# A selective scan whose carried state enters through its input: constant starts, a ring of four input slots, the state copied by another engine

## The chip, the cores and the metric

The kernel runs on one core of a Trainium2 chip. A core has engines that run side by side and wait for each other by semaphores: TensorE (PE, matrix products), VectorE (DVE), ScalarE (ACT), GpSimd (POOL) and SyncE (SP), whose queue issues most of the transfers (DMAs). The metric is the device time of one execution in microseconds (us); lower is better.

## The reference

Two layers over an image of 4 x 512 channels x 64 x 64, so 4 sequences of 4096 positions. The first layer normalizes, cuts the 512 channels into four chunks of 128 and runs one Mamba block over each of the 16 sequences; the second is linear attention. What matters here is the scan of the Mamba block:

```python
A = -jnp.exp(A_log)
def step(h, inp):
    dt_t, B_t, C_t, x_t = inp
    dA = jnp.exp(dt_t[:, :, None] * A)
    h = dA * h + (dt_t * x_t)[:, :, None] * B_t[:, None, :]
    y = jnp.einsum('bds,bs->bd', h, C_t)
    return (h, y)
h0 = jnp.zeros((Beff, D_INNER, D_STATE), x.dtype)
```

D_INNER is 256 and D_STATE is 16, so each position has 4096 states, and the recurrence runs over 4096 positions.

## The kernel before

**Steps.** The work is cut into tiles of T = 512 positions: 4 images x 8 tiles x 4 chunks = 128 steps (b, t, c), in that order. A step has two halves (e = 0, 1; 128 inner channels each), and a half has 8 slots: SLOTS = 16 slots a step, 2048 in all. A slot does two scans of 128 rows x 512 positions; two slots, jj = 0 and 1, make a pair, which is one group q of four states for all 128 channels of the half. The global slot number is g.

**What a slot needs.** Both halves' dt and dt*x go to DRAM (`d_rows`, line 629) and come back spread over the partitions as `d_all` (`spread`, line 633: eight transfers of 256 KB each time, called in slot 1 for half 1 and in slot 9 for half 0 of the next step). `b_all` is one group's rows of B, broadcast over partitions by four transfers of 64 KB (`b_row`, line 692); `c_sb` is the tail of the rows of C (`c_tail`, line 697, four of 16 KB). ACT forms dA = exp(dt * A) into one of three PSUM banks (`decay`, line 708, three scans ahead). POOL forms bx = (dt*x) * B for two scans at once (`drive`, line 717), two slots ahead, into one of three tiles.

**What a slot does** (`slot`, line 725). DVE runs two scans (line 739), h = dA * h + bx along the 512 positions. The scan's starting value is 0.0 in the first tile of an image and a column of `st` later, the state left by the tile before. At the end of a pair POOL copies the last column of h into `st` (line 750) and multiplies the last 128 positions of h by C, in place (line 751); DVE multiplies the first 384 (`product`, line 759), one scan into the next pair; PE sums the states of a channel (`fold_states`, line 761).

**Order.** Inside `manual_schedule` every engine and SP's queue work through their instructions in the order in which the code issues them. A queue whose first instruction must wait holds back all behind it. `after()` (line 1108) places the other work of a step in its slots: the next step's products, `spread`, `gate` (POOL, line 780, slots 1 and 9), `to_rows` (POOL, line 624, slot 4, the product dt*x), the norms and the attention, which are generators that advance a piece at a time as PE's budget allows. In the transfers this gives, per pair: `b_row` for a pair three ahead in the even slot, `c_tail` in the odd one, and `spread` after the `c_tail` of slots 1 and 9. Tiles that share a tag and a number of buffers reuse each other's memory; a new use waits for the old one's last reader.

**Norms.** `layer_norm` (line 419) and `layer_scale` (line 450) work on one tile of positions. Means and variances come from sums over partitions on PE; the temporary tiles all have the tag `sq`, four buffers.

Of the kernel before, what the change touches and what calls it, by code (L numbers as in the profile page):

```python
# [8 lines left out]
F32 = mybir.dt.float32  # L9
# [15 lines left out]
def kernel(  # L25
# [136 lines left out]
    ident = wk.tile([P, P], F32, tag="sq", name="ident", bufs=4)  # L162
# [62 lines left out]
    w_x = wk.tile([P, DI], F32, tag="bx", name="w_x", bufs=3)  # L225
# [37 lines left out]
    a_sb = rows(a_log, wk.tile([P, NH, NST], F32, tag="sq", name="a_sb", bufs=4))  # L263
# [9 lines left out]
    b_qk = wk.tile([P, C], F32, tag="bx", name="b_qk", bufs=3)  # L273
# [15 lines left out]
    a_k = wk.tile([P, NH, KS, NQ], F32, tag="sq", name="a_k", bufs=4)  # L289
# [96 lines left out]
    def mean_of(sums, what, when, stop=True):  # L386

        got = wk.tile([P, T], F32, tag="sq", name=f"got_{what}", bufs=4)
# [14 lines left out]
    def over_deviation(v, var, name):  # L403
        rs = wk.tile([P, T], F32, tag="sq", name=f"rs_{name}", bufs=4)
# [14 lines left out]
    def layer_norm(v, name):  # L419
# [6 lines left out]
        mu = yield from mean_of(sums, f"mu_{name}", "one ahead")  # L426
# [4 lines left out]
        sqs = []  # L431
        for c in range(NC):
            sqs.append(wk.tile([P, T], F32, tag="sq", name=f"sq_{name}_{c}", bufs=4))
            nc.scalar.activation(sqs[c], v[:, c, :], AF.Square)
            if c == 1:
                yield "free"
        yield from room()
        sums = work_bank(f"var_sums_{name}")
        sums_into(sums, sqs, range(NC))
        var = yield from mean_of(sums, f"var_{name}", "two ahead")  # L440
# [9 lines left out]
    def layer_scale(v, name):  # L450
# [8 lines left out]
        mu = yield from mean_of(sums, f"mu_{name}", None)  # L459
        mu2 = wk.tile([P, T], F32, tag="sq", name=f"mu2_{name}", bufs=4)  # L460
# [8 lines left out]
        sqs = [None] * NC  # L469

        def part(c):
            sqs[c] = wk.tile([P, T], F32, tag="sq", name=f"sq_{name}_{c}", bufs=4)
            nc.scalar.activation(sqs[c], v[:, c, :], AF.Square, bias=about)
# [12 lines left out]
        var = yield from mean_of(sums, f"var_{name}", "two ahead", False)  # L486
# [80 lines left out]
    def shifted_end(f, name):  # L567
# [4 lines left out]
        d2 = small.tile([P, NC], F32, tag="d2", name=f"d2_{name}")  # L572
# [110 lines left out]
    b_all, c_all, c_sb, dAs, bxs, hs, ys = {}, {}, {}, {}, {}, {}, {}  # L683
# [8 lines left out]
    def b_row(g):  # L692
        n, e, q, _ = place(g)
        b_all[g // JJ] = wk.tile([P, T], F32, tag="b_all", name=f"b_all_{g}", bufs=3)
# [22 lines left out]
    def drive(g):  # L717

        n, e, q, jj = place(g)
        bxs[g] = wk.tile([P, 2, T], F32, tag="bx", name=f"bx_{g}", bufs=3)  # L720
        nc.gpsimd.tensor_tensor(  # L721
            bxs[g], fs[n]["d_all", e][:, 1, jj * 2 : jj * 2 + 2, :], bc(b_all[g // JJ], 2), ALU.mult
        )

# [515 lines left out]
```

## Time and profile before

| | |
|---|---|
| median of 3 runs | 7956.4 us (7953.15 to 7964.96) |
| profiled execution | 7963.09 us, span 7961.4 us |
| first scan / last scan begins | 122.4 us / 7492.2 us |
| DVE busy | 6977.7 us (88%) |
| POOL busy | 6880.5 us (86%) |
| PE busy | 6453.6 us (81%) |
| ACT busy | 5507.6 us (69%) |
| the hardware DMA queue q1 | 1222.32 MB, 61.1% of the 16 engines' span |
| chain that ended last, by engine | DVE 33%, PE 21%, ACT 15%, DMA 12%, issue 8%, SPq 6%, POOL 6% |

In a group's row of the profile stand the line of the code, the engine, the operation, the tiles written and read, the shapes and the count; then the busy time of the group in us, the mean duration of one in ns, and the time its engine sat idle just before such instructions, with what ended most of that. A row of a timeline is: start in us, time covered in us, engine, line, operation, tiles, shape, and how many instructions were merged into the row; the bracket is idle time and what ended it. Instructions that follow each other on one engine overlap by some 0.05 to 0.1 us, so what one more costs is read from start to start. SPq rows are SP issuing transfers; a row of four issues that waits inside shows as a longer row. A row of waits is: who waited, for what, us in total, times, the longest in us.

### The profile page before, as it was taken

The page shows a single profiled execution, that of the slowest core. Times are in us where ns is not written, and L with a number is a line of the kernel's source. Part 1 is how long each engine was busy: PE and PEld are TensorE (multiplying, and loading weights), DVE is VectorE, ACT ScalarE, POOL GpSimd, SP SyncE. Part 2 cuts the span into 40 slices and gives each one's busy share as a digit, 9 for nine tenths or more (in the row PEclk, how much of TensorE's full clock was granted, in tenths as well). Part 3 has the DMA queues.
Part 4 walks back from the last instruction along what each step waited for, and adds up shares of the span by engine and source line. Part 5 has one row for each costly group of instructions (what it writes and reads, how often), then busy time and mean ns, then how long its engine had stood idle before and what let it go on. Part 6 is the DMA issues. An engine that isn't in the chain of part 4 may idle for free.

```text
span 7961.4 us, 90563 instructions
## 1 busy us (share of the span) xinstructions
PE 6453.6 (81%) x24835; PEld 2120.0 (27%) x24880; DVE 6977.7 (88%) x5766; ACT 5507.6 (69%) x8321; POOL 6880.5 (86%) x4597
## 2 busy tenths in 40 slices
PE   5676777677789888888788888898688888888599
PEld 1121212112223222322222223332122332322144
DVE  5999999999999999989999999998999999988600
ACT  4667777777777777767777777677777777777421
POOL 4999999999999899989999899898999999889600
PEclk7888888888899999998899999899899999999799
DMA  5666666666666666777766666677666666676402
GB/s 154 167 168 166 151 155 159 160 155 167 169 179 162 151 163 159 174 189 175 174 155 171 171 157 161 155 185 189 156 167 163 161 161 159 145 194 180 112 32 90
DMA packets 829184, 1265.87 MB, mean 159 GB/s; under 512 B 183912, under 2 KB 317560, under 8 KB 816384
## 3 DMA queue, kind: packets, MB, share of 16 engines
q1 hardware_dynamic: 804736, 1222.32, 61.1%
q0 software_dynamic: 16896, 33.56, 2.4%
q10 hardware_dynamic: 7040, 4.20, 0.2%
q8 instruction: 195, 3.19, 0.2%
q14 instruction: 317, 2.60, 0.1%
HBM read 1052.78 MB, written 206.57 MB: 158 GB/s over the span
## 4 chain that ended last, share of the span: by engine, by line
DVE 33%; PE 21%; ACT 15%; DMA 12%; issue 8%; SPq 6%; POOL 6%; POOLq 0%; ACTq 0%; DVEq 0%
DVE h L739 22%; DVE h L759 9%; DMA d_all<-d_rows 7%; ACT dA L713 5%; PE pq L124 5%; POOL bx L721 4%; PE pc L124 4%; SPq L688 3%; PE y L124 3%; PE pr L124 3%; SPq L639 2%; DMA c_sb<-c_rows 2%; ACT xz L1048 2%; PE po L124 2%; ACT L1048 1%
## 5 line engine op out<-in xcount | busy, mean ns | idle before, releaser
L721 POOL TENSOR_TENSOR bx<-d_all,b_all 128x1024 f32<-128x1024 f32 x2048 | 4824.7, 2367 | 213.3 <-DVE h L739 195.1
L739 DVE TENSOR_TENSOR_SCAN h<-dA,st,bx 128x512 f32<-128x512 f32 x3584 | 4358.9, 1264 | 358.7 <-ACT dA L713 159.0
L713 ACT ACTIVATE dA<-d_all,a_t 128x512 f32<-128x512 f32 x4096 | 2752.9, 687 | 1568.5 <-DVE h L739 1521.8
L759 DVE TENSOR_TENSOR h<-h,c_all 128x1536 f32<-128x1536 f32 x1024 | 1767.5, 1726 | 0.1
L751 POOL TENSOR_TENSOR h<-h,c_sb 128x512 f32<-128x512 f32 x1024 | 1300.2, 1270 | 190.2 <-DMA c_sb<-c_rows 95.2
L124 PE MATMUL y<-h,fold 128*32 128x512 f32 x8192 | 1271.2, 696 | 71.6 <-POOL h L751 67.4
L124 PE MATMUL c_all<-parts,sel 128*128 128x384 bf16 x1024 | 369.9, 361 | 1123.3 <-DVE h L759 1121.7
L124 PE MATMUL pc<-xn,w_cv 128*128 128x512 f32 x2048 | 1045.7, 645 | 122.8 <-DVE xn L414 62.1
L124 PE MATMUL pq<-w_qk,xa 128*128 128x512 f32 x2048 | 965.5, 604 | 7.9 <-issue 5.3
L739 DVE TENSOR_TENSOR_SCAN h<-dA,bx 128x512 f32<-128x512 f32 x512 | 591.2, 1203 | 90.0 <-ACT dA L713 65.1
L124 PEld LDWEIGHTS <-sel 128*128 128x128 bf16 x1280 | 127.1, 99 | 1762.2 <-DVE h L759 1562.5
L124 PEld LDWEIGHTS pc<-xn,w_cv 128*128 128x128 f32 x2048 | 389.5, 201 | 747.1 <-issue 424.7
L124 PEld LDWEIGHTS pq<-w_qk,xa 128*128 128x128 f32 x2048 | 398.6, 196 | 439.6 <-issue 422.4
L124 PE MATMUL pr<-xb,m 128*128 128x512 f32 x1024 | 485.3, 612 | 7.5 <-DMA xb<-x 3.6
L124 PE MATMUL pp<-xn,w_pr 128*128 128x512 f32 x1024 | 477.7, 597 | 4.8 <-DVE xn L414 4.8
L124 PEld LDWEIGHTS y<-h,fold 128*32 128x32 f32 x8192 | 170.6, 114 | 644.0 <-issue 344.9
L124 PE MATMUL y<-xz,dg 32*32 32x512 f32 x2048 | 337.3, 734 | 0.0
L781 POOL TENSOR_TENSOR xz<-xz 128x512 f32<-128x512 f32 x256 | 325.7, 1272 | 9.2 <-ACT xz L778 9.2
L832 ACT ACTIVATE kq<-pq 128x512 f32<-128x512 f32 x256 | 150.5, 588 | 259.9 <-PE pq L124 259.2
L124 PE MATMUL pd<-xz,w_xp 128*128 128x512 f32 x512 | 323.4, 764 | 7.8 <-ACT xz L1048 7.8
L628 POOL TENSOR_TENSOR dt<-dt,xz 128x1024 f32<-128x1024 f32 x128 | 302.3, 2361 | 24.7 <-ACT dt L620 24.6
L124 PE MATMUL pz<-xn,w_z 128*128 128x512 f32 x512 | 275.4, 631 | 11.7 <-ACT xz L608 8.2
(179 smaller groups left out, 6034.1 us busy)
## 6 DMA issues: line engine op xcount, KB each, us to landing
d_all<-d_rows SPq DMA_DIRECT2D x2048, 256.0 KB, 6.7
b_all<-b_rows SPq DMA_DIRECT2D x4096, 64.0 KB, 2.2
d_rows<-dt SPq DMA_DIRECT2D x256, 512.0 KB, 3.6
c_sb<-c_rows SPq DMA_DIRECT2D x4096, 16.0 KB, 1.8
xs<-in_x_dram SPq DMA_DIRECT2D x32, 1024.0 KB, 6.3
xn<-in_x_dram SPq DMA_DIRECT2D x32, 1024.0 KB, 6.2
xr<-in_x_dram POOLq DMA_DIRECT2D x32, 1024.0 KB, 10.7
x<-xr SPq DMA_DIRECT2D x32, 1024.0 KB, 4.2
```

The costliest lines, as they stand in the source:

```text
L124: nc.tensor.matmul(out_, lhsT, rhs, **how)
L628: nc.gpsimd.tensor_tensor(f["both"][:, 1], f["both"][:, 0], f["xz"][:, 0], ALU.mult)
L639: nc.sync.dma_start(d[k * BLK : (k + 1) * BLK, v], src)
L688: nc.sync.dma_start(dst[k * BLK : (k + 1) * BLK, :], rows_[q * KS + k, :].partition_broadcast(BLK))
L713: nc.scalar.activation(dAs[k], fs[n]["d_all", e][:, 0, j, :], AF.Exp, scale=a_t[:, e, j, q : q + 1])
L721: nc.gpsimd.tensor_tensor(bxs[g], fs[n]["d_all", e][:, 1, jj * 2 : jj * 2 + 2, :], bc(b_all[g // JJ], 2), ALU.mult)
L739: nc.vector.tensor_tensor_scan(h[:, j, :], dAs.pop(2 * g + i), bxs[g][:, i, :], 0.0 if t == 0 else st[:, c, e, q, j : j + 1], ALU.mult, AL ...
L751: nc.gpsimd.tensor_tensor(h[:, :, CUT:], h[:, :, CUT:], bc(c_sb.pop(g // JJ), NJ), ALU.mult)
L759: nc.vector.tensor_tensor(own, own, bc(c_all.pop(g // JJ), NJ), ALU.mult)
L781: nc.gpsimd.tensor_tensor(f["xz"][:, 1, e, :], f["xz"][:, 1, e, :], f["xz"][:, 0, e, :], ALU.mult)
L832: nc.scalar.activation(qk[i], pq, AF.Relu)
L1048: nc.scalar.activation(fs[n]["xz"], fs[n]["xz"], AF.Silu)
```

## The change

Every scan starts at the constant 0.0. The state of the tile before enters instead through bx: the first column of a pair's bx gets `exp(A * dt_first) * st` added, which is what the scan would have made of its starting value. For this a small tile `carry` (128 x 32) is formed per half, in steps with t > 0: `carry_over` (POOL, A times the first column of dt), `carry_decay` (ACT, Exp) and `carry_on` (POOL, times `st`); then one POOL add of 128 x 4 elements follows the second drive of every pair. bx becomes one tile of four slots, `drive` runs three slots ahead (DRIVE = 3), `st` is copied by ACT. Memory for the fourth slot comes from `b_all` (two buffers in place of three, loaded in the odd slot behind `c_tail`, for the pair two ahead), from `sq` (three fixed tiles `sqb` in place of four rotating ones, so that one norm's variance sums are split in two) and from two small tiles. `spread` moves from slot 1 to slot 0 and from slot 9 to slot 7.

```diff
-    b_all, c_all, c_sb, dAs, bxs, hs, ys = {}, {}, {}, {}, {}, {}, {}
+    b_all, c_all, c_sb, dAs, hs, ys = {}, {}, {}, {}, {}, {}
+    RING, DRIVE = 4, 3
+    bx = const.tile([P, RING, 2, T], F32, tag="bx", name="bx")
+    carry = const.tile([P, NH, NJ, NQ], F32, tag="carry", name="carry")
...
     def b_row(g):
         n, e, q, _ = place(g)
-        b_all[g // JJ] = wk.tile([P, T], F32, tag="b_all", name=f"b_all_{g}", bufs=3)
+        b_all[g // JJ] = wk.tile([P, T], F32, tag="b_all", name=f"b_all_{g}", bufs=2)
         for_states(b_all[g // JJ], fs[n]["b_rows"], q)
...
     def drive(g):
 
         n, e, q, jj = place(g)
-        bxs[g] = wk.tile([P, 2, T], F32, tag="bx", name=f"bx_{g}", bufs=3)
         nc.gpsimd.tensor_tensor(
-            bxs[g], fs[n]["d_all", e][:, 1, jj * 2 : jj * 2 + 2, :], bc(b_all[g // JJ], 2), ALU.mult
+            bx[:, g % RING], fs[n]["d_all", e][:, 1, jj * 2 : jj * 2 + 2, :],
+            bc(b_all[g // JJ], 2), ALU.mult,
         )
+        if jj == JJ - 1 and steps[n][1]:
+            if q == 0:
+                carry_on(g)
+            r = (g - jj) % RING
+            first = bx[:, r : r + JJ, :, 0].rearrange("p r i -> p (r i)")
+            nc.gpsimd.tensor_tensor(first, first, carry[:, e, :, q], ALU.add)
+
+    def carry_over(g):
+
+        n, e, _, _ = place(g)
+        nc.gpsimd.tensor_tensor(
+            carry[:, e], a_t[:, e],
+            fs[n]["d_all", e][:, 0, :, 0].unsqueeze(2).to_broadcast([P, NJ, NQ]), ALU.mult,
+        )
+
+    def carry_decay(g):
+        _, e, _, _ = place(g)
+        nc.scalar.activation(carry[:, e], carry[:, e], AF.Exp)
+
+    def carry_on(g):
+        n, e, _, _ = place(g)
+        nc.gpsimd.tensor_tensor(
+            carry[:, e], carry[:, e], st[:, steps[n][2], e].rearrange("p q j -> p j q"), ALU.mult
+        )
+
+    def starts_half(g, last):
+
+        return g < last and g % (SLOTS // NH) == 0 and steps[g // SLOTS][1] > 0
 
     def slot(g, last, after):
         n, e, q, jj = place(g)
         b, t, c = steps[n]
-        if g + 2 < last:
-            drive(g + 2)
+        if starts_half(g + DRIVE + 1, last):
+            carry_over(g + DRIVE + 1)
+        if g + DRIVE < last:
+            drive(g + DRIVE)
         if jj == 0:
-            if g + 3 * JJ < last:
-                b_row(g + 3 * JJ)
             hs[g // JJ] = wk.tile([P, NJ, T], F32, tag="h", name=f"h_{g}", bufs=2)
-        elif g + 1 < last:
-            c_tail(g + 1)
+        else:
+            if g + 1 < last:
+                c_tail(g + 1)
+            if g + 1 + 2 * JJ < last:
+                b_row(g + 1 + 2 * JJ)
         h = hs[g // JJ]
         for i in range(2):
             j = jj * 2 + i
             nc.vector.tensor_tensor_scan(
-                h[:, j, :], dAs.pop(2 * g + i), bxs[g][:, i, :],
-                0.0 if t == 0 else st[:, c, e, q, j : j + 1], ALU.mult, ALU.add,
+                h[:, j, :], dAs.pop(2 * g + i), bx[:, g % RING, i, :], 0.0, ALU.mult, ALU.add,
             )
+            if i == 1 and jj == JJ - 1:
+                nc.scalar.copy(st[:, c, e, q, :], h[:, :, T - 1])
...
-        del bxs[g]
+        if starts_half(g + DRIVE, last):
+            carry_decay(g + DRIVE)
         if jj == JJ - 1:
-            nc.gpsimd.tensor_copy(st[:, c, e, q, :], h[:, :, T - 1])
             nc.gpsimd.tensor_tensor(
                 h[:, :, CUT:], h[:, :, CUT:], bc(c_sb.pop(g // JJ), NJ), ALU.mult
             )
...
-    for g in range(JJ, 3 * JJ, JJ):
-        b_row(g)
+    b_row(JJ)
     c_row(0)
-    for g in range(2):
+    for g in range(DRIVE):
         drive(g)
+    b_row(2 * JJ)
...
-                    if s == 1:
+                    if s == 0:
                         spread(f, 1, nm)
-                        if before is not None:
-                            gate(before, 1)
+                    if s == 1 and before is not None:
+                        gate(before, 1)
...
+                    if s == 7 and nxt is not None:
+                        spread(nxt, 0, names[n + 1])
                     if s == 9:
                         gate(f, 0)
-                        if nxt is not None:
-                            spread(nxt, 0, names[n + 1])
```

In the norms (left out here but for the core):

```diff
-    ident = wk.tile([P, P], F32, tag="sq", name="ident", bufs=4)
+    sqb = const.tile([P, 3, T], F32, tag="sqb", name="sqb")
+    ident = sqb[:, 0, 0:P]
...
-        sqs = []
-        for c in range(NC):
-            sqs.append(wk.tile([P, T], F32, tag="sq", name=f"sq_{name}_{c}", bufs=4))
+        sqs = [sqb[:, i, :] for i in (1, 2, 0, 1)]
+        for c in range(2):
             nc.scalar.activation(sqs[c], v[:, c, :], AF.Square)
-            if c == 1:
-                yield "free"
+        yield "free"
         yield from room()
         sums = work_bank(f"var_sums_{name}")
-        sums_into(sums, sqs, range(NC))
-        var = yield from mean_of(sums, f"var_{name}", "two ahead")
+        sums_into(sums, sqs, (0, 1))
+        for c in range(2, NC):
+            nc.scalar.activation(sqs[c], v[:, c, :], AF.Square)
+        yield "free"
+        sums_into(sums, sqs, (2, 3))
+        var = yield from mean_of(sums, f"var_{name}", "two ahead", 0)
```

More of the change, by code (lines that the diff above doesn't have):

```diff
@@ L224 @@
     w_cv = const.tile([P, NTAP, DI], F32, tag="w_cv", name="w_cv")
-    w_x = wk.tile([P, DI], F32, tag="bx", name="w_x", bufs=3)
+    w_x = wk.tile([P, DI], F32, tag="res", name="w_x", bufs=2)
     nc.scalar.dma_start(w_x, in_w[:, 0:DI])
@@ L262 @@
     skd = const.tile([P, BLK], F32, tag="skd", name="skd")
-    a_sb = rows(a_log, wk.tile([P, NH, NST], F32, tag="sq", name="a_sb", bufs=4))
+    a_sb = rows(a_log, sqb[:, 1, 0 : NH * NST].rearrange("p (e s) -> p e s", e=NH))
     w_op = const_rows(op_w, "w_op")
@@ L272 @@
     bqk = const.tile([P, C], BF16, tag="bqk", name="bqk")
-    b_qk = wk.tile([P, C], F32, tag="bx", name="b_qk", bufs=3)
+    b_qk = wk.tile([P, C], F32, tag="res", name="b_qk", bufs=2)
     nc.vector.memset(b_qk, 0.0)
@@ L286 @@
         nc.vector.tensor_copy(bqk[r, :], b_qk[r, :])
-    a_k = wk.tile([P, NH, KS, NQ], F32, tag="sq", name="a_k", bufs=4)
+    a_k = sqb[:, 2, 0 : NH * NST].rearrange("p (e k q) -> p e k q", e=NH, k=KS)
     nc.scalar.activation(a_k, a_sb.rearrange("p e (q k) -> p e k q", k=KS), AF.Exp)
@@ L384, in sums_into, with mean_of @@
             )
-    def mean_of(sums, what, when, stop=True):
-        got = wk.tile([P, T], F32, tag="sq", name=f"got_{what}", bufs=4)
+    def mean_of(sums, what, when, at, stop=True):
+        got = sqb[:, at, :]
         def take():
@@ L403, in over_deviation @@
     def over_deviation(v, var, name):
-        rs = wk.tile([P, T], F32, tag="sq", name=f"rs_{name}", bufs=4)
+        rs = sqb[:, 2, :]
         def root():
@@ L425, in layer_norm @@
         sums_into(sums, [v[:, c, :] for c in range(NC)], range(NC))
-        mu = yield from mean_of(sums, f"mu_{name}", "one ahead")
+        mu = yield from mean_of(sums, f"mu_{name}", "one ahead", 0)
         yield "wide"
@@ L458, in layer_scale @@
         sums_into(sums, [v[:, c, :] for c in range(NC)], range(NC))
-        mu = yield from mean_of(sums, f"mu_{name}", None)
-        mu2 = wk.tile([P, T], F32, tag="sq", name=f"mu2_{name}", bufs=4)
+        mu = yield from mean_of(sums, f"mu_{name}", None, 0)
+        mu2 = sqb[:, 0, :]
         def square():
@@ L468, in layer_scale @@
         yield from until(squared)
-        sqs = [None] * NC
+        sqs = [sqb[:, i, :] for i in (1, 2, 1, 2)]
         def part(c):
-            sqs[c] = wk.tile([P, T], F32, tag="sq", name=f"sq_{name}_{c}", bufs=4)
             nc.scalar.activation(sqs[c], v[:, c, :], AF.Square, bias=about)
@@ L485, in layer_scale @@
         sums_into(sums, sqs, (2, 3))
-        var = yield from mean_of(sums, f"var_{name}", "two ahead", False)
+        var = yield from mean_of(sums, f"var_{name}", "two ahead", 1, False)
         mm(var, minus_first.to_broadcast([P, P]), mu2, start=False, stop=True)
@@ L571, in shifted_end @@
         nc.vector.tensor_scalar(mv, mv, 1.0 / L, None, ALU.mult)
-        d2 = small.tile([P, NC], F32, tag="d2", name=f"d2_{name}")
+        d2 = small.tile([P, NC], F32, tag="d2", name=f"d2_{name}", bufs=1)
         nc.vector.tensor_tensor(d2, mv[:, :, 0], mv[:, :, 0], ALU.mult)
@@ L896, in attention @@
         nc.gpsimd.memset(kqn, 0.0)
-        nrm = small.tile([P, NC], F32, tag="nrm", name=f"nrm_{b}")
+        nrm = small.tile([P, NC], F32, tag="nrm", name=f"nrm_{b}", bufs=1)
         nc.vector.tensor_reduce(nrm, kq, AX.X, ALU.add)
```

## The prediction

> **What bounds the kernel now.** I read the groups by cost first, then the waits, then the timelines of DVE, POOL and SP's queue over one stretch.
>
> ```profile
> span 7961.4 us, 90563 instructions
> L721 POOL TENSOR_TENSOR bx<-d_all,b_all 128x1024 f32<-128x1024 f32 x2048 | 4824.7, 2367 | 213.3 <-DVE h L739 195.1
> L739 DVE TENSOR_TENSOR_SCAN h<-dA,st,bx 128x512 f32<-128x512 f32 x3584 | 4358.9, 1264 | 358.7 <-ACT dA L713 159.0
> L739 DVE TENSOR_TENSOR_SCAN h<-dA,bx 128x512 f32<-128x512 f32 x512 | 591.2, 1203 | 90.0 <-ACT dA L713 65.1
> ```
>
> The loop of 2048 slots runs from 122 to 7494 us, 7371 us, 57.6 per step of 16 slots; about 590 us lie outside it. Inside, DVE is busy 6914 us and POOL 6867: two engines at 93%, each idle for some 460 to 510 us. A change must help both, or it moves the bound to the other.
>
> ```profile
> 4024.81 1.73 DVE L759 TENSOR_TENSOR h<-h,c_all 128x1536 f32<-128x1536 f32 x1
> 4026.45 4.80 DVE L739 TENSOR_TENSOR_SCAN h<-dA,st,bx 128x512 f32<-128x512 f32 x4
> 4031.17 1.73 DVE L759 TENSOR_TENSOR h<-h,c_all 128x1536 f32<-128x1536 f32 x1
> ```
> ```profile
> 4021.44 2.35 POOL L721 TENSOR_TENSOR bx<-d_all,b_all 128x1024 f32<-128x1024 f32 x1 [0.16 <-DVE h L739]
> 4023.78 0.19 POOL L750 COPY st<-h 128x4 f32<-128x4 f32 x1
> 4024.05 1.27 POOL L751 TENSOR_TENSOR h<-h,c_sb 128x512 f32<-128x512 f32 x1
> 4025.28 2.36 POOL L721 TENSOR_TENSOR bx<-d_all,b_all 128x1024 f32<-128x1024 f32 x1
> 4027.81 2.37 POOL L721 TENSOR_TENSOR bx<-d_all,b_all 128x1024 f32<-128x1024 f32 x1 [0.17 <-DVE h L739]
> ```
>
> A pair of slots (one b_all tile, four scans) takes DVE 6.36 us (4024.81 to 4031.17) without a gap. POOL needs start to start 2.34 + 0.27 + 1.23 + 2.36 = 6.2 us, and waits 0.17 for the scan that frees a bx buffer. They are level.
>
> SP's queue is the third clock. After every spread (eight d_all transfers of 256 KB, twice per step) the transfers behind it are issued slowly:
>
> ```profile
> 4024.05 1.76 SPq L688 DMA_DIRECT2D b_all<-b_rows  x4
> 4025.90 1.76 SPq L688 DMA_DIRECT2D c_sb<-c_rows  x4
> 4027.76 3.70 SPq L639 DMA_DIRECT2D d_all<-d_rows  x8
> 4031.56 3.79 SPq L688 DMA_DIRECT2D b_all<-b_rows  x4
> 4036.26 4.07 SPq L688 DMA_DIRECT2D c_sb<-c_rows  x4
> 4040.43 1.91 SPq L688 DMA_DIRECT2D b_all<-b_rows  x4
> ```
> ```profile
> SPq L688 <- DMA d_all<-d_rows: 1555.2, 1736, 3.9
> ```
>
> Four issues cost 1.76 us when nothing holds them, 3.8 and 4.07 behind a spread; 1736 waits over 256 spreads are about seven of the next eight. So the first four behind a spread are out 7.6 us after it began (4035.35), the next four 12.6 us after (4040.33). This costs almost nothing today, since b_all is loaded long ahead.
>
> **The change, part by part.**
>
> *Scans.* 3584 scans lose the st operand. Start to start: 4.72 us for four with st (4026.45 to 4031.17) is 1.18 each; in the first tile, where the start is already constant, four take 143.72 to 148.20, 4.48, or 1.12. 60 ns x 3584 = 215 us off DVE's busy time, which the means (1264 less 1203, 61 ns) repeat. That is the whole possible gain; it is time only where DVE ends last.
>
> *st copy.* POOL loses 1024 copies of 0.27 us start to start (4023.78 to 4024.05): 276 us. ACT gains them and 224 carry_decay; ACT has no 128x4 copy, so between the 0.19 of its accumulator read and the 0.47 of a 32x384 cast; I take 0.22: 275 us. ACT idles 1522 us before L713, waiting for the scans, which hides it; without that cover each copy would hold back a decay, 275 us. The tail product L751 overwrites h, so it now waits for ACT's copy. POOL's copy waited for the scan only 79 times in 1024, 79 us, so the scan is normally long over; I price this at 0 to 150 us and take 20. The Trainium skill (ScalarE: Activation LUTs, "What ACT_TABLE_LOAD costs") has 186 ns + 0.833 ns per element, an estimate of 0.19 us for this copy; no run here shows it, and by it the sum would stay.
>
> *Small adds on POOL.* 896 adds, 224 carry_over, 224 carry_on. No small POOL multiply or add is shown; the rows at 512 elements (1270 ns) and 1024 (2367) extrapolate to 0.17 at none, and the copy has 0.20. Below is 0.15 (a pad copy's pitch, 4010.13 to 4010.28), above 1.04 (the 128x4 power). I take 0.30 for the add, since it waits for its own drive to complete as L751 waits 0.08 for the st copy, and 0.15 and 0.20 for the others: 269 + 34 + 45 = 348 us against 276 removed, net +72 (bounds -75 and +1100; the upper row is a power, so I stay at the copy).
>
> *Ring and lead.* drive runs three slots ahead in four buffers: drive(g+3) overwrites what scan g-1 read, the same release as now, so it adds no wait. An even slot waits for drive(g+3) plus add where it waited for one drive: no lead gained there, one slot on odd ones. DVE waits only 78 us for bx today.
>
> *b_all, the costly part.* Three buffers become two, and its load is issued after c_tail, in the odd slot. Today the load for a pair may start once drive(g+1) is done and is needed by drive(g+6); in the new one it is released by drive(g+2) and needed by drive(g+5): two slots less. The spreads move too (after slot 0 and 7 instead of 1 and 9), so SP's order becomes b_all, spread, c_sb, b_all: the needed b_all is now in the *second* four behind the spread. Count from the end of the drive that releases the b_all ahead of the spread (4021.44 + 2.35 = 4023.79): 0.26 + 1.76 + 0.1 until the spread starts (2.1), 12.6 until the last of the second four is issued, 2.2 landing (median of b_all): 16.9 us. POOL's own work from there to the drive that needs it (a drive behind a drive is 2.31: 4.67 for two in the timeline, less 2.36): add 0.3, drive 2.31, tail 1.23, drive 2.31, add 0.3, drive 2.31, tail 1.23, gate 1.23, drive 2.31, add 0.3 = 13.8 us. In today's trace the same stretch takes 15.7 us on average, 14.5 without the one tail that the new order moves out of it. So POOL stands 16.9 - 14.5 = 2.4 us per spread, x256 = 614 us.
>
> POOL cannot win that back: its pair is 6.15 us afterwards and DVE's 6.1, so what is late next is the drive, then the scan, then product and fold. DVE's 215 us become waiting. SP's chain alone also gives a floor: per step 2 x 16.9, plus POOL's work outside the two stretches, 14.5 (with the dt product of 2.31) and 12.2, is 60.5 us, against 57.6 now.
>
> The Trainium skill speaks for the other side. DMA: Bandwidth & Descriptors ("Anatomy of one DMA") fits a transfer as 2.0 us plus bytes over 436 GB/s, an estimate of 6.8 us for a 2 MB spread. The rows show its last four lanes free only after 12.6. By the page b_all would be in at about 11 us, under the 13.8, and nothing would stand; the rows decide.
>
> *The rest.* The three fixed sq slots split one norm's variance sums into two groups, each as long as the one now (1.06 us for mu_sums in the timeline): 34 us of PE over 32 tiles, hidden as PE is not the bound; one slot more of latency for a norm that has several steps of room. d2, nrm, and the setup tiles: nothing, they run a few times. carry_over needs d_all one slot before the drive; d_all has landed by then (spread start + 13, needed 15 or more later).
>
> **The sum**, on the execution of 7961.4: + 614 (b_all) + 34 (carry_over, outside the stretches) + 20 (tail behind ACT) - 95 (L751's waits for c_sb, which the standing covers) + 0 (DVE) = +573, 8535. The spread often starts late: other loads sit before it. Each 0.1 us adds 26 us; I add 0.1, and predict 8560. The execution lies 5 us above the median of 7956.4, which I neglect.
>
> **Rivals.**
> 1. *The load is in time* (faster). Decides: the needed b_all lands within 14 us of the release; SP would have to issue c_sb and b_all without the lane waits. For it: DVE idles 457 us partly for others, and POOL's lead grows. Against: the 3.8 and 4.07 us groups. Then, each engine ending last in half of the loop, half of DVE's 215 is won and half of POOL's 72 paid: 7961 - 108 + 36 = 7889.
> 2. *Half of it stands.* Spreads start at once and lanes free over a microsecond early: 15.5 needed, 1.0 x 256 = 256, so 8217. For it: some spreads are shorter. Against: other loads in the queue.
> 3. *ACT or the ring serializes.* If the ring were tracked as one tile, each scan would wait for the newest drive: a pair of some 11 us, past 11000; today's scans that read st do not wait for the copy of a neighbouring slice (5.6 us in 7 waits), which speaks against it. Milder: the tail waits for ACT behind table loads (1.28 us each, four per step) and costs 1.0 us a pair: 1024 us on top of the forecast, 9580.
>
> **Numbers.** Forecast 0.75, rival 1 0.10, rival 2 0.10, rival 3 0.05. The range 8200 to 8850 takes in rival 2 and a spread 1.1 us later (+290); what a measurement here can tell from no change is about 0.2%. Faster 0.09, same 0.03, slower 0.88.
>
> **What would show it.** Right: POOL bx waiting for b_all, some 250 times at 2 to 4 us, before the drives of slots 6 and 14; DVE waiting for POOL bx; scans at 1203 ns. SP's queue with c_sb, then b_all behind each spread. Wrong: bx waits for b_all under 100 us, or POOL's wait at L751 on ACT's st above 200.

## The result, and the profile after

The changed kernel takes 8832.1 us (median of 4 runs, 8811.3 to 8837.7) against 7954.8 beside it (4 runs): a ratio of 1.110 (95% interval 1.108 to 1.112). It is slower, by 877 us where the forecast had 604. The profiled execution grew by 869 us, from a span of 7961.4, and 864 of these lie in the loop of slots, which went from 7371 to 8235 us (57.6 to 64.3 per step).

The page of the changed kernel: the chain that ended last by engine, and the groups by cost.

```profile
span 8830.6 us, 91929 instructions
...
DMA 30%; PE 19%; POOL 14%; issue 11%; SPq 10%; DVE 9%; ACT 6%; POOLq 0%; ACTq 0%; DVEq 0%
...
L775 DVE TENSOR_TENSOR_SCAN h<-dA,bx 128x512 f32<-128x512 f32 x4096 | 4774.6, 1207 | 1409.0 <-POOL bx L734 854.8
L725 POOL TENSOR_TENSOR bx<-d_all,b_all 128x1024 f32<-128x1024 f32 x2048 | 4860.4, 2375 | 1035.1 <-DMA b_all<-b_rows 646.1
...
L788 POOL TENSOR_TENSOR h<-h,c_sb 128x512 f32<-128x512 f32 x1024 | 1316.2, 1285 | 168.7 <-ACT st L779 137.7
```

All 4096 scans now take 1207 ns, as the first tile's did before, so the part of the change that was to save DVE time does. But the chain, in which DVE led with 33%, is now led by transfers (30%). The idle time ahead of `drive` (line 725) rose from 213 to 1035 us, the scans' own idle from 449 (two groups) to 1409, mostly waiting for POOL's small add (line 734). The saving has become waiting.

The profile also shows a lower granted TensorE clock (0.868 of full speed over the span, 0.897 before), and PE is busy 242 us longer. No run fixes the clock, so a share of it in the loss is not excluded; but PE's share of the chain fell from 21% to 19%, and the loss per step is there at both levels of the clock: 7.7 us in the first image (0.82 before, 0.79 after), 6.5 in the other three (0.92 and 0.89).

POOL's waits (who, for what, us in total, times, longest):

```profile
POOL bx L725 <- DMA b_all<-b_rows: 646.1, 170, 10.7
POOL bx L725 <- DMA c_sb<-c_rows: 256.4, 65, 13.4
POOL h L788 <- ACT st L779: 137.7, 88, 5.5
POOL bx L725 <- DVE h L775: 55.1, 22, 6.8
```

`drive` does not read `c_sb`. The second row is most likely the same wait as the first, put down to the transfer that the profile saw last. So the waits are better counted by place: of the drives, those for slot 6 stood 126 times, 617.6 us in all (4.9 each), those for slot 14 stood 122 times, 346.1 us (2.8 each). That is 964 us in exactly the two places that the prediction names. The third row is new, the tail product held by ACT's copy: 138 us; the waits of that line for c_sb, 95.2 us before, are down to 4.

How `drive` comes to wait for b_all is seen in SP's queue and POOL's timeline over the same stretch, first for slot 14 (rows to 4084), then for slot 6.

```profile
4067.22 1.69 SPq L693 DMA_DIRECT2D b_all<-b_rows  x4
4069.01 3.70 SPq L641 DMA_DIRECT2D d_all<-d_rows  x8
4072.80 0.53 SPq L1018 DMA_DIRECT2D out_dram<-res  x1
4074.12 3.92 SPq L693 DMA_DIRECT2D c_sb<-c_rows  x4
4079.07 3.10 SPq L693 DMA_DIRECT2D b_all<-b_rows  x4
...
4097.37 0.36 SPq L661 DMA_DIRECT2D b_rows<-dt  x1
...
4102.43 4.25 SPq L641 DMA_DIRECT2D d_all<-d_rows  x8
4107.50 3.90 SPq L693 DMA_DIRECT2D c_sb<-c_rows  x4
4112.36 3.86 SPq L693 DMA_DIRECT2D b_all<-b_rows  x4
```
```profile
4064.83 2.36 POOL L725 TENSOR_TENSOR bx<-d_all,b_all 128x1024 f32<-128x1024 f32 x1
...
4079.32 2.35 POOL L725 TENSOR_TENSOR bx<-d_all,b_all 128x1024 f32<-128x1024 f32 x1
4081.75 0.21 POOL L734 TENSOR_TENSOR bx<-bx,carry 128x4 f32<-128x4 f32 x1
4084.18 2.35 POOL L725 TENSOR_TENSOR bx<-d_all,b_all 128x1024 f32<-128x1024 f32 x1 [2.22 <-DMA c_sb<-c_rows]
...
4095.03 2.37 POOL L725 TENSOR_TENSOR bx<-d_all,b_all 128x1024 f32<-128x1024 f32 x1
...
4117.94 2.35 POOL L725 TENSOR_TENSOR bx<-d_all,b_all 128x1024 f32<-128x1024 f32 x1 [5.80 <-DMA b_all<-b_rows]
```

The drive at 4064.83 is that of slot 9; its end (4067.19) frees a b_all buffer, and SP issues into it at once (4067.22). The spread starts 1.8 us after the release, then come c_sb and the b_all that slot 14 needs, whose last transfer is issued at 4082.17, 15.0 us after the release. The drive of slot 14 begins at 4084.18, 17.0 after the release; POOL had finished everything else at 4081.96 and stood 2.2 us. For slot 6 the release is the end of the drive at 4095.03, so 4097.40. Here `b_rows` and `c_rows` (lines 661 and 662, written to DRAM by SP), the c_sb queued behind them and an output also stand between the release and the spread, which starts only 5.0 us after the release; the drive comes 20.5 us after it and has stood 5.8.

Over all steps (medians, counted in the trace): for slot 14 the spread starts 1.8 us after the release, the last b_all is issued at 15.0, the drive starts at 16.8; for slot 6 it is 2.6, 17.4 and 19.8. The slot-6 stand depends on the chunk: 7.1, 3.7, 3.1 and 5.5 us (means) for c = 0 to 3, against 3.0, 2.4, 2.7 and 2.8 for slot 14. Chunk 0 is where a 1 MB load of `xn` lies in the same queue (6.2 us from issue to landing before, 11.8 after), and chunk 3 where POOL issues the 1 MB load of `xr` (line 534) on a queue of its own. Sorted by these loads, the drive of slot 6 comes 14.7 us after the spread's start in the 62 steps in which no 1 MB transfer is issued from 2.5 us before the release to the last b_all, 18.0 in the 24 with `xn` alone and 18.6 in the 29 with `xr` alone; for slot 14 it is 14.8 in the 118 steps without one.

The tail product's wait for ACT has less to do with table loads here than with the norms: 77 of the 138 us lie in the pair that ends with slot 13, 61 of them directly behind a square (line 440) that waited for PE, and 19 in the pair of slot 11, behind the silu and its table loads. ACT's row, and one case in ACT's timeline and POOL's:

```profile
ACT sqb L440 <- PE var_sums_a L124: 170.7, 32, 7.1
```
```profile
1443.21 0.63 ACT L440 ACTIVATE sqb<-xn 128x512 f32<-128x512 f32 x1 [5.86 <-PE var_sums_a L124]
```
```profile
1444.62 1.26 POOL L788 TENSOR_TENSOR h<-h,c_sb 128x512 f32<-128x512 f32 x1 [2.86 <-ACT st L779]
```

The fourth square of a norm goes into the fixed `sqb` slot of the first, so it waits until PE has summed that one; a decay and the copy of st stand behind it. The kernel before has no such wait at its squares (line 434).

The small operations, in the view of POOL's groups with shapes kept apart:

```profile
L734 POOL TENSOR_TENSOR bx<-bx,carry 128x4 f32<-128x4 f32 x896 | 187.0, 209 | 70.2
L750 POOL TENSOR_TENSOR carry<-carry,st 128x16 f32<-128x16 f32 x224 | 52.9, 236 | 0.0
L739 POOL TENSOR_TENSOR carry<-a_t,d_all 128x16 f32<-128x16 f32 x224 | 49.9, 223 | 0.0
```

The 896 adds took 187.0 busy and 70.2 idle ahead of them, 257 us (269 forecast); the two products 103 (79 forecast).

The account of the loop, on POOL:

| | forecast, us | measured, us |
|---|---|---|
| `drive` stands for b_all, slots 6 and 14 | 614 + 26 for a late spread | 964 |
| the tail product stands for ACT's copy of st | 20 | 138 |
| its waits for c_sb | -95 | -92 |
| POOL's busy time | 34 (carry_over; the rest inside the stretch) | 87 |
| `drive` waiting for a scan to free bx | 0 | -140 (195.1 to 55.1) |
| the st copy waiting for the scan | 0 | -79 (the copy has gone) |
| sum | 599 | 878, where the loop grew by 864 |

### The profile page after: what moved, and what is told of

It is laid out like the page before. It is cut to its first block, busy times and chain, and to the rows that moved or that the text cites. A ratio compares the mean times of both kernels' runs of the same rounds, so it can differ in the third digit from the quotient of the medians.

```text
span 8830.6 us, 91929 instructions
## 1 busy us (share of the span) xinstructions
PE 6695.7 (76%) x24835; PEld 2160.4 (24%) x24880; DVE 6806.0 (77%) x5766; ACT 5628.6 (64%) x9569; POOL 6967.6 (79%) x4917
## 3 DMA queue, kind: packets, MB, share of 16 engines
q1 hardware_dynamic: 804736, 1222.32, 55.1%
## 4 chain that ended last, share of the span: by engine, by line
DMA 30%; PE 19%; POOL 14%; issue 11%; SPq 10%; DVE 9%; ACT 6%; POOLq 0%; ACTq 0%; DVEq 0%
DMA d_all<-d_rows 17%; POOL bx L725 8%; POOL h L788 5%; SPq L641 5%; DVE h L775 5%; SPq L693 4%; DMA c_sb<-c_rows 4%; DMA b_all<-b_rows 4%; PE pq L124 3%; PE y L124 3%; DMA xn<-in_x_dram 3%; PE pd L124 3%; DVE h L796 2%; PE pr L124 2%; ACT dA L718 2%
## 5 line engine op out<-in xcount | busy, mean ns | idle before, releaser
L775 DVE TENSOR_TENSOR_SCAN h<-dA,bx 128x512 f32<-128x512 f32 x4096 | 4774.6, 1207 | 1409.0 <-POOL bx L734 854.8
L725 POOL TENSOR_TENSOR bx<-d_all,b_all 128x1024 f32<-128x1024 f32 x2048 | 4860.4, 2375 | 1035.1 <-DMA b_all<-b_rows 646.1
L718 ACT ACTIVATE dA<-d_all,a_t 128x512 f32<-128x512 f32 x4096 | 2787.1, 687 | 1576.4 <-DVE h L775 1467.2
L124 PE MATMUL y<-h,fold 128*32 128x512 f32 x8192 | 1336.0, 730 | 869.0 <-POOL h L788 862.6
L124 PE MATMUL pc<-xn,w_cv 128*128 128x512 f32 x2048 | 1027.4, 635 | 85.4 <-DVE xn L415 52.5
L124 PE MATMUL pd<-xz,w_xp 128*128 128x512 f32 x512 | 389.7, 904 | 7.8 <-ACT xz L1085 7.8
L630 POOL TENSOR_TENSOR dt<-dt,xz 128x1024 f32<-128x1024 f32 x128 | 302.0, 2359 | 20.5 <-ACT dt L622 20.5
L876 DVE TENSOR_TENSOR kq<-pk,kq 128x256 f32<-128x256 f32 x124 | 50.8, 410 | 311.2 <-PE pk L124 311.2
L124 PE MATMUL po<-xz,w_op 128*128 128x512 f32 x512 | 288.7, 690 | 2.0 <-POOL xz L818 2.0
## 6 DMA issues: line engine op xcount, KB each, us to landing
xn<-in_x_dram SPq DMA_DIRECT2D x32, 1024.0 KB, 11.8
```

The costliest lines, as they stand in the source:

```text
L124: nc.tensor.matmul(out_, lhsT, rhs, **how)
L630: nc.gpsimd.tensor_tensor(f["both"][:, 1], f["both"][:, 0], f["xz"][:, 0], ALU.mult)
L718: nc.scalar.activation(dAs[k], fs[n]["d_all", e][:, 0, j, :], AF.Exp, scale=a_t[:, e, j, q : q + 1])
L725: nc.gpsimd.tensor_tensor(bx[:, g % RING], fs[n]["d_all", e][:, 1, jj * 2 : jj * 2 + 2, :], bc(b_all[g // JJ], 2), ALU.mult,)
L775: nc.vector.tensor_tensor_scan(h[:, j, :], dAs.pop(2 * g + i), bx[:, g % RING, i, :], 0.0, ALU.mult, ALU.add,)
L876: nc.vector.tensor_tensor(kq, pk, kq, ALU.add)
```

## The experiments

Each kernel ran beside the kernel before on the same chip (its medians lie between 7955 and 7964 us). Where a diff is against the changed kernel it says "after", else "before".

**Cut the spread in two** (after: the four transfers of dt stay after slots 0 and 7, the four of dt*x follow two slots later).

```diff
-    def spread(f, e, nm):
+    def spread(f, e, nm, vs=(0, 1)):
...
-        for v in range(2):
+        for v in vs:
...
-                    if s == 0:
-                        spread(f, 1, nm)
+                    if s in (0, 2):
+                        spread(f, 1, nm, (s // 2,))
...
-                    if s == 7 and nxt is not None:
-                        spread(nxt, 0, names[n + 1])
+                    if s in (7, 9) and nxt is not None:
+                        spread(nxt, 0, names[n + 1], (s // 9,))
```

> The changed kernel with each spread cut in two: the four transfers of dt where the change put all eight (after slots 0 and 7), the four of dt*x two slots later (after slots 2 and 9). Theory (b_all is late because it stands behind eight spread transfers): it now stands behind four; released at 0, spread begun at 2, four lanes free by 8, landed at 10 to 12 us, under POOL's 13.8. POOL's waits before the drives of slots 6 and 14 fall from 964 us to under 150, and the time to 7900 to 8100. Rival A (the loss is POOL's and ACT's new small work, the tail's wait for ACT's copy): unchanged, 8780 to 8850. Rival B (the bytes of the spread delay everything behind them, however they are cut): half of it, about 8400.

8185.7 us, ratio 1.028 (1.027 to 1.030): 646 us of the 877 are gone, with every other part of the change in place. SP's queue and POOL's waits in this kernel:

```profile
4023.01 1.79 SPq L643 DMA_DIRECT2D d_all<-d_rows  x4
4024.90 1.76 SPq L694 DMA_DIRECT2D c_sb<-c_rows  x4
4027.08 3.62 SPq L694 DMA_DIRECT2D b_all<-b_rows  x4
4030.75 1.84 SPq L643 DMA_DIRECT2D d_all<-d_rows  x4
```
```profile
POOL h L789 <- ACT st L780: 221.2, 125, 5.1
POOL bx L726 <- DMA b_all<-b_rows: 133.5, 81, 14.5
```

Behind four bulk transfers c_sb is issued in 1.76 us, unhindered, and b_all is out 7.7 us after the spread began (4030.70) where it took 13.2 for slot 14 in the changed kernel (4082.17 less 4069.01). The stands before slots 6 and 14 fell from 964 to 91 us. So the late b_all is most of the loss. The time lies above what was expected, because with that wait gone another grows: the tail product behind ACT's copy (138 to 221 us). Counted by place, whatever the profile names as the cause, the tail product stands 222 us, 123 times, in the pair that ends with slot 11, where it stood 28 us in the changed kernel.

**Issue b_all ahead of c_sb** (after).

```diff
+            if g + 1 + 2 * JJ < last:
+                b_row(g + 1 + 2 * JJ)
             if g + 1 < last:
                 c_tail(g + 1)
-            if g + 1 + 2 * JJ < last:
-                b_row(g + 1 + 2 * JJ)
```

> The changed kernel with b_row issued ahead of c_tail in the odd slot; nothing else. Theory: b_all moves from the second four behind the spread to the first, issued by 7.6 us after the spread's begin and landed at about 13 instead of 15 us: 1.5 to 3 us less in each of 256 stretches, 8100 to 8450, and SP's timeline shows b_all directly behind d_all. Rival A (small work, ACT's copy): 8780 to 8850. Rival C (the lateness is SP waiting for ACT and PE before it gets to b_all at all): under 100 us won, above 8730.

8935.1 us, ratio 1.123 (1.121 to 1.124), 103 us slower than the changed kernel: a miss, with the stands before slots 6 and 14 up from 964 to 1087 us. The time lies in rival C's range, but its reason does not show for slot 14: SP goes from the spread to b_all without waiting for ACT or PE. The queue and POOL for a spread before slot 14:

```profile
4050.15 1.72 SPq L693 DMA_DIRECT2D b_all<-b_rows  x4
4051.92 1.99 SPq L693 DMA_DIRECT2D c_sb<-c_rows  x4
4054.02 3.75 SPq L641 DMA_DIRECT2D d_all<-d_rows  x8
4057.89 4.80 SPq L693 DMA_DIRECT2D b_all<-b_rows  x4
```
```profile
4047.77 2.36 POOL L725 TENSOR_TENSOR bx<-d_all,b_all 128x1024 f32<-128x1024 f32 x1
...
4067.83 2.36 POOL L725 TENSOR_TENSOR bx<-d_all,b_all 128x1024 f32<-128x1024 f32 x1 [3.61 <-DMA b_all<-b_rows]
```

b_all is the first group behind the spread, and its last transfer is issued 12.6 us after the release (4062.69 less 4050.13) instead of 15.0. It still lands only 13.8 us after the spread began (4067.83), and c_sb, which used to go out before the release, now stands between the release and the spread, which starts 3.9 us after it instead of 1.8. The drive comes 17.7 us after the release; it had been 17.0. So more than the turn to be issued holds b_all: it lands behind the spread's bytes. The spread's own last transfer lands 12.7 us after its start (median of the transfers whose landing the trace has), b_all 13.9 here and 14.9 in the changed kernel, though its last transfer is out 8.7 us after the spread's start in the rows here (4062.69 less 4054.02) and 13.2 there. With half the bytes ahead, in the kernel with the cut spread, it lands 9.6 us after the start of the first part (slot 14).

The slow issue behind a spread comes from how the program counts its transfers. SP's transfers use eight semaphores in turn, and an issue does not end before the transfer eight places ahead has landed (in all 4147 cases whose landing the trace has). So the last of the second four behind a spread is out only when the spread's last transfer has landed, which is why the 12.6 us that the prediction took for that issue and the landing of the spread agree.

**b_all's two buffers alone** (before: two buffers, loaded in the odd slot behind `c_tail`; spreads, starts and copies untouched).

```diff
-        ... bufs=3)
+        ... bufs=2)
...
         if jj == 0:
-            if g + 3 * JJ < last:
-                b_row(g + 3 * JJ)
...
-        elif g + 1 < last:
-            c_tail(g + 1)
+        else:
+            if g + 1 < last:
+                c_tail(g + 1)
+            if g + 1 + 2 * JJ < last:
+                b_row(g + 1 + 2 * JJ)
```

> The kernel before with one part of the change alone: two b_all buffers, loaded in the odd slot behind c_tail for the pair two ahead. Scans, st copy, bx, spreads and norms as before. Theory: this part alone costs nearly all: 8500 to 8850, with POOL's bx waiting for b_all before the drives of slots 8 and 0, behind the spreads of slots 1 and 9. Rival A: under 8100.

8087.2 us, ratio 1.016 (1.015 to 1.018): 129 us, far under what was expected and in the rival's range. POOL's waits, and the first of these rows in the kernel before:

```profile
POOL h L752 <- DMA c_sb<-c_rows: 296.1, 165, 9.8
POOL bx L721 <- DMA b_all<-b_rows: 13.4, 15, 2.8
```
```profile
POOL h L751 <- DMA c_sb<-c_rows: 95.2, 63, 6.6
```

Here b_all is in time. The release is now the end of the drive of slot 3 and the need that of slot 8, two slots ahead: between them lie three tail products instead of two, and in one half the product dt*x of line 628 as well. What is late is c_sb, now with b_all in the same slot (95 to 296 us). So two buffers in the old order are not enough for the loss. Whether the loss needs them is not shown: no run has the new places of the spread with three buffers.

**Spreads back after slots 1 and 9** (after).

```diff
-                    if s == 0:
+                    if s == 1:
                         spread(f, 1, nm)
...
-                    if s == 7 and nxt is not None:
+                    if s == 9 and nxt is not None:
                         spread(nxt, 0, names[n + 1])
```

> The changed kernel with the spreads back in the slots of before (after 1 and 9). Theory (what counts is the work that POOL still has between the release of one b_all and the drive that needs the one queued behind the spread): the wanted b_all is now that of slots 8 and 0; POOL's work on the way is 16.3 us in half 1, since the dt product of slot 4 lies in it, and 14.0 in half 0, against 16.9 for the chain of SP and transfers. Waits for b_all fall from 964 to 350 to 550 us, most of them before slot 0; time 8250 to 8450. Rival (the place of the spread does not matter): 8780 to 8850.

8363.5 us, ratio 1.051 (1.049 to 1.053), as expected: 469 us back from two changed numbers.

```profile
POOL bx L725 <- DMA b_all<-b_rows: 236.8, 158, 5.9
POOL h L788 <- ACT st L779: 231.3, 163, 4.9
```

The stands moved to slots 0 (193 us) and 8 (133), and those before 6 and 14 are gone (3 us). So the place of the spread is a cause. How it works differs by half, counted from the release (medians). For slot 8, POOL is done with its other work after 16.4 us, where it was 14.1 for slot 6, since the product dt*x of slot 4 now lies in the stretch; and the drive comes after 17.3 us instead of 19.8, as the long chains of c = 0 and 3 are gone (14.9 and 15.5 us from the spread's start to the drive, where slot 6 had 18.2 and 18.6). For slot 0, POOL is done after 15.5 us, where it was 14.1 for slot 14, and the drive comes after 17.1, where it was 16.8: the stretch now holds the tail product of slot 11, which stands behind ACT, so one wait hides part of the other.

**`b_rows` and `c_rows` written later** (after: `later(1, rows_out)` becomes `later(4, rows_out)`), to see whether SP's wait for ACT's dt, 41.5 us before and 307.9 after, is why slot 6 stands longer.

> The changed kernel with the two small stores of B and C rows issued three slots later (after slot 1 of the next step and behind its b_all, in place of slot 14). Theory: SP's 308 us of waiting for ACT's dt copy stands in front of the b_all and the spread of half 1 and makes its chain 19.8 us where half 0 has 16.8; without it the wait before slot 6 falls from 618 us to 350 to 450, before slot 14 it stays near 346; time 8580 to 8700. Rival (half 1 is longer for other transfers on the queue): 8800 to 8840.

8774.3 us, ratio 1.102 (1.100 to 1.103): 58 us, less than expected. The spread for slot 6 now starts 1.8 us after the release, as for slot 14, but the drive still comes 19.3 after it, and the stands for slot 6 are 554 us. So the late start is a small part; the rest is time behind the spread's start. By chunk they are 6.8 us for c = 0 and 4.7 for c = 3, 3.0 and 2.8 for the two others, and the steps sort by the 1 MB loads as in the changed kernel (14.8 us from the spread's start to the drive without one, 18.3 with `xn`, 18.7 with `xr`). None of these loads was taken away, so this rests on the comparison of steps within a trace.

**No carried state** (after: `carry_over`, `carry_decay`, `carry_on` and the adds left out).

```diff
-        if jj == JJ - 1 and steps[n][1]:
+        if False:
...
-        return g < last and g % (SLOTS // NH) == 0 and steps[g // SLOTS][1] > 0
+        return False
```

> The changed kernel without carry_over, carry_decay, carry_on and the small adds; the carried state is left out. It takes 290 us of busy time and 70 us of waiting off POOL. Theory: three of four adds lie in stretches in which POOL stands anyway; what is won is the work outside them, about 0.5 us in each of 224 halves, 110 us: 8690 to 8780. Rival A (POOL's small work costs in full): 360 us, about 8470.

8800.3 us, ratio 1.105 (1.104 to 1.107). 360 us of POOL's work and its waits are out, and 32 come back, where 110 were expected: the stands before slots 6 and 14 grow from 964 to 1166. POOL comes sooner to a b_all that is no earlier. In the changed kernel the small operations cost little, since POOL stands anyway.

**Constant starts alone** (before, all scans start at 0.0, the carried state left out).

> The kernel before with every scan started at the constant 0.0 and nothing else changed; the carried state is left out, so tiles after the first forget it. It prices the scans alone: DVE's busy time falls by 215 us. Theory (DVE and POOL end last in about half of the loop each): 70 to 110 us less, 7845 to 7885. Rival D (DVE alone bounds the loop): 215 less, 7740. Rival E (POOL alone): 7955, same.

7886.5 us, ratio 0.991 (0.989 to 0.992): 72 us gained, at the low end of the 70 to 110 that were expected. The scans of this kernel:

```profile
L739 DVE TENSOR_TENSOR_SCAN h<-dA,bx 128x512 f32<-128x512 f32 x4096 | 4745.2, 1207 | 566.3 <-ACT dA L713 237.6 <-POOL bx L721 132.7 <-PE y L124 98.6
```

DVE is busy some 205 us less (4358.9 + 591.2 before), and a third of it becomes time. This is what the constant starts are worth when nothing is paid for them.

**st copied by ACT alone** (before).

```diff
+            if i == 1 and jj == JJ - 1:
+                nc.scalar.copy(st[:, c, e, q, :], h[:, :, T - 1])
...
         if jj == JJ - 1:
-            nc.gpsimd.tensor_copy(st[:, c, e, q, :], h[:, :, T - 1])
```

> The kernel before with st copied by ACT and nothing else. POOL loses 276 us of work; the tail product now waits for ACT's copy. In the changed kernel that wait is 138 us, and 222 us where the spread was cut in two, nearly all behind ACT's silu and table loads of slot 10. Theory: POOL's relief and that wait about cancel, as DVE is level with POOL: 7900 to 7990. Rival (the tail behind ACT is a loss by itself): above 8030. Rival (POOL bounds): below 7850.

8022.9 us, ratio 1.008 (1.006 to 1.009): 59 us above the kernel before beside it, between the two expectations. POOL has 188 us less work (6880.5 to 6692.3 busy) and yet the kernel is slower:

```profile
POOL h L752 <- ACT st L744: 405.9, 254, 6.0
```

Counted by place, the tail product stands 337 us, 126 times, in the pair that ends with slot 11; 98 of these stands, 257 us, are in the row above. One of them, in POOL's timeline and ACT's:

```profile
4019.59 1.26 POOL L752 TENSOR_TENSOR h<-h,c_sb 128x512 f32<-128x512 f32 x1 [2.92 <-ACT st L744]
```
```profile
4014.18 1.28 ACT L1049 ACT_TABLE_LOAD   x1
4015.48 1.91 ACT L1049 ACTIVATE xz<-xz 128x2048 f32<-128x2048 f32 x1
4017.41 1.28 ACT L1150 ACT_TABLE_LOAD   x1
4018.70 0.69 ACT L713 ACTIVATE dA<-d_all,a_t 128x512 f32<-128x512 f32 x1
4019.33 0.18 ACT L744 COPY st<-h 128x4 f32<-128x4 f32 x1
```

The copy itself takes 0.18 us. It is queued behind a table load, the silu of a whole step, the load back and a decay, 5.2 us in all; POOL's tail product stood for 2.9 of them.

**That one pair back on POOL** (the kernel with the cut spread; ACT copies st except in the pair that ends with slot 11).

```diff
-            if i == 1 and jj == JJ - 1:
+            if i == 1 and jj == JJ - 1 and g % SLOTS != 11:
                 nc.scalar.copy(st[:, c, e, q, :], h[:, :, T - 1])
...
         if jj == JJ - 1:
+            if g % SLOTS == 11:
+                nc.gpsimd.tensor_copy(st[:, c, e, q, :], h[:, :, T - 1])
```

> The changed kernel with the spreads cut in two as in e1_split (8186 us), and the copy of st given back to POOL in the one pair that ends with slot 11, behind ACT's silu and table loads of slot 10. Theory (the second loss is the tail product waiting for ACT's copy: 221 us in e1_split, 123 of its waits in that pair): those waits fall below 40 us, POOL takes 128 copies of 0.27 us, 35 us: 8020 to 8110. Rival (the wait is only moved, since DVE or PE is late there anyway): 8160 to 8200.

8083.2 us, ratio 1.017 (1.014 to 1.019), as expected: 102 us less than with the cut spread alone. POOL's waits:

```profile
POOL bx L726 <- DMA b_all<-b_rows: 166.5, 117, 14.7
POOL h L791 <- ACT st L780: 128.9, 87, 5.3
```

None of the second row lies in the pair of slot 11 any more, but it fell only to 129 us, not below 40: 85 us of it lie in the pair of slot 13, where squares of the norms still wait for PE. 124 us remain above the kernel before, near what two b_all buffers cost alone (129); that it is the same 129 was not tested. What shows in this trace is DVE waiting 314 us for POOL's add, and POOL's two rows above. The granted clock is back at 0.898.

**The same split of the copies, before** (all pairs but that of slot 11 on ACT).

> The kernel before with st copied by ACT in seven of eight pairs, by POOL in the pair that ends with slot 11. ACT's copy in all pairs gave 8023 us, 406 us of tail waits, 337 of them in that pair. Theory: without these POOL keeps most of its relief of 240 us and about half shows, as with the scans: 7820 to 7920, faster than before. Rival (POOL's relief is worth nothing because DVE ends last): 7940 to 7980.

7950.8 us (12 runs), ratio 0.9995 (0.9985 to 1.0005): no gain, where one was expected; the time is in the rival's range. Where the copy is not stuck behind table loads, moving it neither costs nor gains. POOL is busy 154 us less, but its tail product stands 452 us where it stood 115 before: 166 for ACT's copy and 148 for c_sb. So POOL's relief became waiting.

**The cut spread, before** (dt after slots 1 and 9, dt*x after 3 and 11; nothing else of the change).

```diff
-                    if s == 1:
-                        spread(f, 1, nm)
+                    if s in (1, 3):
+                        spread(f, 1, nm, (s // 2,))
...
-                        if nxt is not None:
-                            spread(nxt, 0, names[n + 1])
+                    if s in (9, 11) and nxt is not None:
+                        spread(nxt, 0, names[n + 1], (s // 11,))
```

> The kernel before with its spreads cut in two: dt after slots 1 and 9 as now, dt*x two slots later. Theory: c_sb and b_all stand behind four transfers in place of eight; the tail's waits for c_sb (100 us) go, nothing else of b_all's was waited for: 7880 to 7950. Rival (dt*x lands too late for the first drive of a half): POOL waits for d_all, above 8000.

7921.5 us (6 runs), ratio 0.996 (0.994 to 0.997), as expected: 0.4% under the kernel before, a small gain with the interval clear of 1. POOL's waits of this kernel:

```profile
POOL bx L722 <- DVE h L740: 218.7, 334, 6.6
...
POOL h L752 <- DMA c_sb<-c_rows: 9.1, 6, 4.1
```

The tail product's waits for c_sb, 95.2 us before, are 9.1: the small transfers get in between the two parts.

**Both together** (the last two).

> The kernel before with both: spreads cut in two as in e11 (7922 us) and st copied by ACT but for the pair of slot 11 as in e10 (7951 us, no gain). Theory (DVE ends last there, POOL's 240 us of relief stay unused): 7900 to 7930, within 0.3% of e11. Rival (with c_sb in time POOL's relief shows): 7780 to 7880.

7913.1 us (6 runs), ratio 0.994 (0.993 to 0.996): as expected, not to be told apart from the cut spread alone, and the lowest time that computes everything.

## Why the prediction was right, and where it was off

- **The direction and the mechanism held.** `drive` stands for b_all before slots 6 and 14, 248 times where "some 250" were named (at 2.8 us for slot 14, inside the 2 to 4 us forecast, and 4.9 for slot 6, above it); cutting the spread takes 646 us away with everything else in place. DVE's saving became waiting: 855 us of DVE's idle time is for POOL's add.
- **SP's chain was right for one half and too short for the other.** 16.9 us were worked out from release to use; slot 14 has 16.8 and a stand of 2.8 (2.4 forecast), slot 6 has 19.8 and 4.9. The mis-sized term is the 614 us: it took each of the 256 spreads for the same, with 0.1 us for a late start. The measured sum is 964, and 272 of the 350 over forecast (617.6 less 346.1) are the difference between the halves. The writing of `b_rows` ahead of the spread explains a small part (58 us, by moving it); most of the rest lies in the steps in which a 1 MB load of `xn` or `xr` is issued in the stretch. The other 78 are POOL, which is done with its other work 14.1 us after the release in both halves: near the 13.8 that the prediction counted, not the 14.5 that it then used.
- **One link of that chain is only half of the cause.** The prediction has b_all late since it is in the second four behind the spread, each held back in its issue. The hold is real, by the eight semaphores. But put in the first four b_all was issued 2.4 us sooner after the release and used no sooner, 17.7 us after it: it lands behind the spread's bytes. The number came out right because in the changed kernel both limits fall on the same moment, the landing of the spread's last transfer.
- **The Trainium skill's fit of one transfer** (DMA: Bandwidth & Descriptors, "Anatomy of one DMA") made 6.8 us of a 2 MB spread, an estimate. The page gives the fit for a single transfer issued by GpSimd; a spread is eight transfers on SP's queue, and its last one landed 12.6 to 12.7 us after its start here. The rows were the right choice.
- **The lead was the right thing to count.** Two buffers alone cost 129 us, the old places of the spread give 469 back. Between the release and the use POOL has 13.8 us of work in the new order by the forecast, 14.1 measured; with the two buffers alone, in the old order, it has a tail product more, and the product dt*x besides in one half.
- **The tail behind ACT was mis-sized**: 20 us forecast from a bound of 0 to 150, 138 measured. The reason for the low value, that the scan is normally long over, says nothing of ACT's own queue. The third rival named the table loads; they bite in one pair of eight, not in each, and in the changed kernel POOL's stand for slot 14 comes just ahead of that pair's tail product and hides most of it. In the kernel before, ACT's copy alone costs 59 us.
- **The norms were put at nothing, and are not.** The prediction has the three fixed sq slots hidden, as PE is not the bound. It did not count that ACT works in order: a square that waits for PE holds up the copy of st behind it, and through it POOL (61 of the 138 us in the changed kernel). What these slots cost in time is not shown, since no run gives the rotating buffers back.
- **The total is closer than its terms.** The stands and the tail overran the forecast by 442 us together; two waits that the forecast left as they were went away and take 219 back (140 for a scan to free bx, 79 of the copy). Without them the account would end above the stated range, and with them the time lies near its top. That it lies inside is in part luck.
- **The small operations** were priced well (257 against 269 us for the adds, 103 against 79 for the products) and mostly hidden: without them 32 us come back. The ACT copy was taken at 0.22 us; it took 0.19.
- **The Trainium skill's estimate for that copy** (ScalarE: Activation LUTs, "What ACT_TABLE_LOAD costs") was 0.19 us, which the 190 ns of the 1024 copies bear out.
- **Rival 1 would have been wrong twice.** The load was late; and where it is nearly in time, with the cut spread and the pair of slot 11 mended, the kernel is still 1.7% slower than before. The gain of constant starts alone is 72 us.
- **Of the signs named**, the wait on ACT's st stayed under the 200 that would have spoken against the forecast, and rose above it (221 and 231 us) in the two kernels where b_all stands less: one wait covered part of the other.

Open: what keeps the mended version 124 us above the kernel before (its trace shows POOL standing 167 us for b_all and 129 for ACT's copy), and how much the 1 MB loads of `xn` and `xr` cost, since none was moved.

## What to carry to other kernels

A buffer taken from a load's ring is paid in lead. Count, in the consumer's own work, how long it is from the release to the use, and against it the queue's whole chain, with the bytes of the bulk transfers ahead; then do it for each place in the loop, since not every step has the same neighbours in the queue. Where small urgent loads share a queue with bulk ones, cut the bulk: here that removed three quarters of the loss, and made the kernel before 0.4% faster too. A copy that is moved to a less busy engine takes on that engine's queue, table loads included, and whoever overwrites the source waits for it. Buffers taken from a third place, here the norms, can make that queue wait too.

## What the hardware showed unexpectedly

- Issuing a small transfer earlier behind bulk ones on one queue hardly brought it in earlier: b_all's landing moved from 14.9 to 13.9 us after the spread's start, when it went from the second group of four to the first. The spread's own last transfer, 2 MB in all, landed at 12.6 to 12.7.
- A scan of 128x512 that starts from a column is 57 ns longer than one that starts from a constant (means of 1264 and 1207 ns).
- A POOL product or add of 128x4 takes 209 ns and one of 128x16 223 to 236, next to 2375 at 128x1024: none went under some 0.2 us.
